# Seventeen of 25 node tiles reach their two experts through lists of places, with the expert's number in a register

## The chip, the core and the metric

The kernel runs on one core of a Trainium2 chip, as one launch. The metric is the device time of an execution in microseconds. Three runs of the kernel before took 2793.08, 2795.08 and 2800.14 us; their median is 2795.08. The profile comes from one further execution, which took 2804.75 us.

## The reference

The input is a graph of 3125 nodes with 512 features and 53,125 edges. A graph-attention network of two layers and a linear-attention mixer are added to the input; on the sum works a mixture of experts, and this is the part that the change is about:

```python
logits = xf @ Wg + bg                       # xf: layer norm of the 3125 rows
probs = softmax(logits, axis=-1)            # 8 experts
_, top_idx = top_k(probs, 2)
comb = probs * mask_of(top_idx)             # two weights a row are not zero
out = zeros_like(xf)
for e in range(8):
    h = gelu(xf @ W1[e] + b1[e])            # 512 -> 128
    y = h @ W2[e] + b2[e]                   # 128 -> 512
    out = out + comb[:, e:e + 1] * y
```

The reference computes every expert for every row and multiplies six of the eight results by zero. Everything is float32. The output is the sum plus this result.

## The kernel before

**Tiles and groups.** The nodes are sorted by their degree and cut into 25 tiles (`TILES`): 24 of 128 rows and one of 53. `FGROUPS` joins them in groups of four tiles; group 6 is the 53-row tile alone. The features of a group lie in `xT`, features by partition, rows along the free axis.

**The program.** A first part sorts the nodes and makes the tables of neighbours. Two attention layers follow, each with its feed-forward part and batch norm; they take the time up to about 2320 us of the profile. The last stage is the function `last`. The order of each engine's instructions is made by a scheduler from the order in which the program states them and from what they depend on, so that neighbouring pieces of the program interleave.

**The last stage.** `gates(t0, k)` is a generator that works on one group in five steps:

- four transposes a tile turn `xT` into rows, ScalarE copies them into `yall` (L1002), VectorE takes their statistics (L468, L469);
- two gathers a tile by indirect DMA on GpSimd fetch the rows of `base` and `xb` (L1012), GpSimd adds them (L1015), VectorE normalizes and adds (L1017, L1019) and takes statistics again;
- the normalized row `z` (L1028) is turned back into features (`to_features`: four transposes, and a copy that VectorE and ScalarE make in turns), and four matmuls with 8 columns give the gate's logits (L1033, L1035);
- softmax and the rank of each of the 8 weights (L1040 to L1058) leave two weights a row;
- the weights are transposed to `combT` (L1063, L1065).

`expert_sums(t0, k, ahead)` then adds the two biases `b2` by one matmul a tile (L1074, L1076), and for each of the 8 experts makes four matmuls of 512 columns into `ph` (L1080), a Gelu with the bias `b1` on ScalarE (L1083), and for each tile one matmul of 512 columns into `py` (L1087), which VectorE weighs and adds to `yall` (L1089). After each expert it asks the generator of the next group for one step, so that the gates of the next group stand beside the experts of this one. At the end GpSimd puts each tile's rows to their nodes' places in `out` by an indirect DMA (L1095). The groups come in the order 6, 5, 0, 1, 2, 3, 4 (L1100).

**Queues.** DMAs that `nc.sync` issues go out from SP, those of `nc.gpsimd` from GpSimd. In the last stage SP has only the loads of the experts' weights, issued ahead of it (`load_experts`), and GpSimd has the gathers, the additions of L1015 and the puts. Tiles of a pool have a fixed number of places (`bufs`), and a new use waits for the readers of the old one.

Of the kernel before, what the change touches and what calls it, by code (L numbers as in the profile page):

```python
# [53 lines left out]
assert FT == 25 and EP * EQ == NE and max(CAPS) < min(DEGS, PAD) and len(CAPS) == FT  # L54

# [354 lines left out]
def listed_layers(ctx: ExitStack, tc: tile.TileContext, rows,  # L410
# [553 lines left out]
    def load_experts(fp):  # L964
        w1t = fp.tile([128, NX, NP, FX], F32, name="w1t")
        w2t = fp.tile([FX, NX, D], F32, name="w2t")
        for e in range(NX):
            nc.sync.dma_start(w1t[:, e], w1[e].rearrange("(c p) f -> p c f", p=128))
            nc.sync.dma_start(w2t[:, e, :], w2[e])
        b2t = fp.tile([NX, D], F32, name="b2t")  # L970
        nc.sync.dma_start(b2t, b2)
        wgt = fp.tile([128, NP, NX], F32, name="wgt")
        nc.sync.dma_start(wgt, wg.rearrange("(c p) e -> p c e", p=128))
        bgt = fp.tile([P, NX], F32, name="bgt")
        nc.sync.dma_start(bgt, rows_by_partition(bg, 0, P))
        gt = fp.tile([P, D], F32, name="gt")
        nc.sync.dma_start(gt, rows_by_partition(rows, ROW_G, P))
        return w1t, w2t, b2t, wgt, bgt, gt


    def last(xT, w1t, w2t, b2t, wgt, bgt, gt):
        with tc.tile_pool(name="fin", bufs=1, reuse_waits="tile") as fp, \
                tc.tile_pool(name="fin_p", bufs=2, space=PSUM, reuse_waits="tile") as pp:
            yall = fp.tile([P, FT, D], F32, name="yall")
            puts, gated = [], {}

            def gates(t0, k):


                tiles = TILES[t0:t0 + k]  # L990
                mv = fp.tile([P, GT, 2], F32, name="mv1", bufs=2)
                mv2 = fp.tile([P, GT, 2], F32, name="mv2", bufs=2)
                prob = fp.tile([P, GT, NX], F32, name="prob", bufs=3)
# [32 lines left out]
                for i, (t, n) in enumerate(tiles):  # L1026
                    z = fp.tile([P, D], F32, name="z", bufs=3)
                    nc.vector.tensor_scalar(z[:n], yall[:n, t, :], mv2[:n, i, 0:1], sd[:n, i:i + 1],  # L1028
                                            op0=OP.subtract, op1=OP.mult)
                    to_features(pp, "tr", xT[:, :, t * P:t * P + n], z, n)  # L1030
                    pg = pp.tile([P, NX], F32, name="pg", bufs=1)
                    for c in range(NP):
                        nc.tensor.matmul(pg[:n], lhsT=xT[:, c, t * P:t * P + n], rhs=wgt[:, c, :],  # L1033
                                         start=(c == 0), stop=(c == NP - 1))
                    nc.vector.tensor_add(prob[:n, i, :], pg[:n], bgt[:n])  # L1035
                yield

                m = fp.tile([P, GT], F32, name="pm", bufs=2)
                wide = [P, GT, NX]
# [7 lines left out]
                rank = fp.tile(wide, F32, name="rank", bufs=2)  # L1047
                nc.vector.memset(rank, 0.0)
                for e in range(NX):
                    more = fp.tile(wide, F32, name="more", bufs=2)  # L1050
                    pe = prob[:, :, e:e + 1]
                    nc.vector.tensor_tensor(more[:, :, :e + 1], pe.to_broadcast([P, GT, e + 1]),
                                            prob[:, :, :e + 1], OP.is_gt)
                    if e + 1 < NX:
                        nc.vector.tensor_tensor(more[:, :, e + 1:], pe.to_broadcast([P, GT, NX - 1 - e]),
                                                prob[:, :, e + 1:], OP.is_ge)
                    nc.vector.tensor_add(rank, rank, more)
                nc.vector.scalar_tensor_tensor(prob, rank, 1.5, prob, op0=OP.is_lt, op1=OP.mult)  # L1058
                yield
                combT = fp.tile([NX, GT * P], F32, name="combT", bufs=2)  # L1060
# [5 lines left out]
                gated[t0] = prob, combT  # L1066

            def expert_sums(t0, k, ahead):
                prob, combT = gated.pop(t0)
                gs = slice(t0 * P, min(N, (t0 + k) * P))  # L1070
                w = gs.stop - gs.start
                for i, (t, n) in enumerate(TILES[t0:t0 + k]):
                    pb = pp.tile([P, 512], F32, name="pb", tag="py", bufs=3)
                    nc.tensor.matmul(pb[:n], lhsT=combT[:, i * P:i * P + n], rhs=b2t,  # L1074
                                     start=True, stop=True)
                    nc.vector.tensor_add(yall[:n, t, :], yall[:n, t, :], pb[:n])  # L1076
                for e in range(NX):
# [4 lines left out]
                    hT = fp.tile([FX, GT * P], F32, name="hT", bufs=3)  # L1082
# [8 lines left out]
                    next(ahead, None)  # L1091
                for _ in ahead:
                    pass
                for t, n in TILES[t0:t0 + k]:
                    puts.append(nc.gpsimd.indirect_dma_start(  # L1095
                        out=out, out_offset=bass.IndirectOffsetOnAxis(ap=node(t), axis=0),
                        in_=yall[:n, t, :], in_offset=None))


            groups = FGROUPS[-1:] + [FGROUPS[g] for g in FORDER if g != len(FGROUPS) - 1]  # L1100
            for _ in gates(*groups[0]):
                pass
            for i, g in enumerate(groups):
                expert_sums(*g, gates(*groups[i + 1]) if i + 1 < len(groups) else iter(()))
# [619 lines left out]
```

## Time and profile before

The profiled execution took 2804.75 us, and the span of its instructions is 2803.0 us; the median of the three runs is 2795.08 us.

| | whole span, 2803.0 us | last stage, 2330 to 2803 us |
|---|---|---|
| TensorE busy | 2398.1 us (86%) | 452.7 us (96%) |
| VectorE busy | 2054.1 us (73%) | 295.4 us (62%) |
| ScalarE busy | 1406.5 us (50%) | 108.4 us (23%) |
| GpSimd busy | 1414.4 us (50%) | 97.7 us (21%) |
| granted TensorE clock | 0.91 | 0.92 |
| DMA engines, mean share | | 12% |

A group's row in the profile names the line of the program, the engine, the operation, output and inputs, the shape and the count; then the busy time and the mean of one in ns; then the idle time just before these instructions and what ended it. A float32 matmul leaves two records. Records of TensorE overlap, so that the distance between two starts is what a matmul costs in a stream. A row of the timeline has the start, the length and the instruction, with equal neighbours merged. The granted clock is the share of full speed that the TensorE was given. "Landing" is the time from a DMA's issue to its arrival: 2.7 us for a put of L1095, 3.6 and 3.5 for the gathers of L1012, 2.7 for the write of a 256 KB tile by SP early in the program.

### The profile page before, as it was taken

What the parts mean: (1) busy time and instruction counts of PE and PEld (TensorE: products, weight loads), DVE (VectorE), ACT (ScalarE), POOL (GpSimd) and SP (SyncE); (2) the same over time, 40 slices, a digit from 0 to 9 for tenths busy, and PEclk for the clock granted to TensorE, in tenths of its full rate; (3) what the DMA queues carried; (4) which work ended last, traced back from release to release, by engine and by line L of the source; (5) the groups of instructions that cost most, each with busy time, mean ns of one, the idle gap of its engine ahead of it and who ended that gap; (6) DMA issues with size and microseconds to landing.
All of it is one profiled execution on the core that took longest, in us unless ns stands there. A gap on an engine that the chain in (4) does not pass through costs nothing. (4 is left out here: it accounts for less than half of the span.)

```text
span 2803.0 us, 30800 instructions
## 1 busy us (share of the span) xinstructions
PE 2398.1 (86%) x8935; PEld 1302.4 (46%) x8935; DVE 2054.1 (73%) x3186; ACT 1406.5 (50%) x5315; POOL 1414.4 (50%) x1153
## 2 busy tenths in 40 slices
PE   6987989889889876999697787979888486999998
PEld 3442445545455543344344555555555344444443
DVE  7810999999999985500679888989988566666663
ACT  1111568787776763200276767776767423222220
POOL 3362778888777770011657766676765323222100
PEclk9998999999999987999798888989999796999999
DMA  8434999999999984321869888989887441111000
GB/s 287 171 121 138 328 331 337 332 330 338 330 326 325 332 266 159 122 108 78 286 234 335 287 299 292 329 303 331 309 307 269 131 135 51 34 48 48 32 19 20
DMA packets 214478, 620.58 MB, mean 221 GB/s; under 512 B 48068, under 2 KB 53569, under 8 KB 210199
## 3 DMA queue, kind: packets, MB, share of 16 engines
q0 software_dynamic: 161696, 518.18, 52.4%
q1 hardware_dynamic: 50048, 95.36, 9.4%
q10 hardware_dynamic: 2556, 4.97, 0.5%
q8 instruction: 75, 1.23, 0.2%
q14 instruction: 103, 0.84, 0.1%
HBM read 543.80 MB, written 74.75 MB: 221 GB/s over the span
## 5 line engine op out<-in xcount | busy, mean ns | idle before, releaser
L583 POOL DMA_INDIRECT lane<-kvd,idx x906 | 1147.7, 1267 | 526.7 <-issue 179.7
L624 ACT ACTIVATE lane<-lane,sc 128x64 f32<-128x64 f32 x3888 | 945.4, 339 | 117.9 <-DVE sc L614 117.6
L588 DVE TENSOR_TENSOR lane<-lane,q 128x1024 f32<-128x1024 f32 (+1 forms) x464 | 549.0, 1193 | 161.8 <-DMA lane<-kvd,idx 146.7
L644 PE MATMUL agg<-ident,lane 128*128 128x128 f32 (+1 forms) x3272 | 531.6, 301 | 140.5 <-DVE lane L627 59.5
L644 PEld LDWEIGHTS agg<-ident,lane 128*128 128x128 f32 (+1 forms) x3272 | 424.2, 154 | 316.1 <-ACT lane L624 143.5
L589 DVE TENSOR_REDUCE sc<-lane 128x16 f32<-128x1024 f32 (+1 forms) x464 | 545.5, 1187 | 2.6 <-ACT lane L624 1.6
L627 DVE TENSOR_TENSOR lane<-lane,sc 128x1024 f32<-128x1024 f32 (+1 forms) x214 | 252.3, 1197 | 0.1
L1089 DVE SCALAR_TENSOR_TENSOR yall<-py,prob,yall 128x512 f32<-128x512 f32 (+1 forms) x200 | 148.8, 748 | 112.4 <-PE py L1087 100.8
L555 PE MATMUL pq<-wq,xg 128*128 128x512 f32 (+1 forms) x400 | 201.7, 634 | 18.5 <-ACT kt L734 12.2
L701 PE MATMUL po<-aT,wo 128*128 128x512 f32 (+1 forms) x448 | 194.2, 572 | 20.3 <-ACT aT L688 13.4
L1087 PE MATMUL py<-w2t,hT 128*128 128x512 f32 (+1 forms) x400 | 188.7, 610 | 1.8 <-ACT hT L1083 0.8
L1080 PE MATMUL ph<-xT,w1t 128*128 128x512 f32 x320 | 156.3, 630 | 0.0
L1095 POOL DMA_INDIRECT out<-yall,rec x25 | 25.0, 1001 | 252.3 <-DVE yall L1089 247.4
L1083 ACT ACTIVATE hT<-ph,colt 128x512 f32<-128x512 f32 (+1 forms) x56 | 35.4, 633 | 211.0 <-PE ph L1080 210.8
L494 POOL DMA_INDIRECT kvd<-kv,rec x25 | 24.7, 989 | 222.8 <-DVE kv L491 216.8
L491 DVE COPY kv<-pv 128x512 f32<-128x512 f32 (+1 forms) x25 | 17.3, 692 | 153.4 <-PE pv L488 153.4
L701 PEld LDWEIGHTS po<-aT,wo 128*128 128x128 f32 x448 | 80.3, 202 | 97.9 <-issue 64.9
L1087 PEld LDWEIGHTS py<-w2t,hT 128*128 128x128 f32 (+1 forms) x400 | 71.9, 189 | 101.3 <-issue 69.0
L555 PEld LDWEIGHTS pq<-wq,xg 128*128 128x128 f32 (+1 forms) x400 | 73.4, 199 | 92.8 <-issue 68.3
L372 ACT COPY kv<-pkv 128x512 f32<-128x512 f32 (+1 forms) x50 | 29.2, 585 | 163.8 <-PE pkv L370 136.4
L1012 POOL DMA_INDIRECT bt<-base,rec x25 | 26.8, 1072 | 160.1 <-DVE yall L1019 150.3
L370 PE MATMUL pkv<-wk,xT 128*128 128x512 f32 (+1 forms) x200 | 100.7, 637 | 5.8 <-ACT kv L372 5.8
(264 smaller groups left out, 3288.4 us busy)
## 6 DMA issues: line engine op xcount, KB each, us to landing
lane<-kvd,idx POOLq DMA_INDIRECT x906, 6.3
kvd<-kv SPq DMA_DIRECT2D x24, 512.0 KB, 2.7
zT<-ztd SPq DMA_DIRECT2D x48, 256.0 KB, 5.3
xmid<-xg SPq DMA_DIRECT2D x10, 1024.0 KB, 5.7
xT<-xmid POOLq DMA_DIRECT2D x10, 1024.0 KB, 10.3
xr<-in_x SPq DMA_DIRECT2D x24, 256.0 KB, 3.9
xb<-xo SPq DMA_DIRECT2D x24, 256.0 KB, 5.6
zd<-z SPq DMA_DIRECT2D x24, 256.0 KB, 2.7
```

What stands on the lines that cost most here:

```text
L370: nc.tensor.matmul(ps[:n], lhsT=xT[t][:, c, :n], rhs=wkv[name][:, c, :], start=(c == 0), stop=(c == NP - 1))
L555: nc.tensor.matmul(ps[:n], lhsT=of_place(t, c), rhs=wq[:, c, :], start=(c == 0), stop=False)
L583: gets.append(nc.gpsimd.indirect_dma_start(out=kv[:n, k, :], out_offset=None, in_=kvd[l][:, :], in_offset=bass.IndirectOffsetOnAxis(ap=idx ...
L588: nc.vector.tensor_mul(ks, ks, self.q[:n, None, :].to_broadcast([n, g, D]))
L589: nc.vector.tensor_reduce(self.sc[:n, :, j:j + g].rearrange("p h g -> p g h"), ks.rearrange("p g (h d) -> p g h d", h=H), AX.X, OP.add)
L624: nc.scalar.activation(v[:, k, h, :], v[:, k, h, :], AF.Copy, scale=self.sc[:n, h, j + k:j + k + 1])
L627: nc.vector.tensor_mul(v, v, self.sc[:n, :, j:j + g].rearrange("p h g -> p g h")[:, :, :, None] .to_broadcast([n, g, H, DH]))
L644: nc.tensor.matmul(self.agg[:, c * n:(c + 1) * n], lhsT=kv[:n, k, c * 128:(c + 1) * 128], rhs=ident[:n, :n], is_transpose=True, start=firs ...
L701: nc.tensor.matmul(ps[:, :w], lhsT=wo[:, kk, c * 128:(c + 1) * 128], rhs=aT[gi][:, kk, :w], start=(kk == 0), stop=(kk == NP - 1))
L1080: nc.tensor.matmul(ph[:, :w], lhsT=w1t[:, e, c, :], rhs=xT[:, c, gs], start=(c == 0), stop=(c == NP - 1))
L1087: nc.tensor.matmul(py[:n], lhsT=hT[:, i * P:i * P + n], rhs=w2t[:, e, :], start=True, stop=True)
L1089: nc.vector.scalar_tensor_tensor(yall[:n, t, :], py[:n], prob[:n, i, e:e + 1], yall[:n, t, :], op0=OP.mult, op1=OP.add)
```

## The change

Tiles 0 to 15 and tile 24 (`LISTED`, 2101 rows) no longer go through all experts. Groups 5 and 4 (`ALL_EXPERTS`), tiles 16 to 23, still do.

- While the gates of all other groups run, the eight experts of group 5 are stated between them, one after every third step of the gates. The bias term (L1074, L1076) has become the last step of `gates`. The weights and ranks of the listed tiles are kept in `lprob` and `lrank`, and their rows `z` are also written to DRAM (`zld`) by SP.
- `lists()` counts for each expert how many rows chose it, gives every choice a place (experts one after another, each beginning at a multiple of 128), and makes three tables: `placei`, the two places of each row; `which`, the row that stands at each place, by 34 one-hot matmuls; `experti`, the expert of each part of 128 places. There are 40 parts (`PARTS`: (2 x 2101 + 8 x 127) / 128, rounded down), whatever the data.
- Group 4 has its gates and three experts stated after that.
- `one_expert(part, e, which)`, 40 times: GpSimd gathers the 128 rows of a part, four transposes and a ScalarE copy make features of them, four matmuls of 128 columns and one for the bias `b1` make `ph`, ScalarE the Gelu, one more transpose and a VectorE copy turn `h`, one matmul of 512 columns makes `py`, VectorE copies it, SP writes it to DRAM (`yld`). The weights are addressed by a register `e`, loaded for eight parts at a time.
- Then come the other five experts of group 4, and at the end each listed tile fetches its two rows by two gathers (34 in all), weighs and adds them on VectorE and is put to `out`.

Buffers of `xT` whose content is no longer needed serve as room for these tables and rows. The three places of `z` also serve for `y1`, `hT` has two places in place of three and `combT` one in place of two. `b1t`, a copy of `b1` on one partition, comes by way of DRAM. The core of the diff:

```diff
+ALL_EXPERTS = [FGROUPS[STAY[0]], FGROUPS[4]]
+LISTED = [t for g in FGROUPS if g not in ALL_EXPERTS for t in TILES[g[0]:g[0] + g[1]]]
+NL = len(LISTED)
+PARTS = (2 * sum(n for _, n in LISTED) + NX * (P - 1)) // P
...
+                    if listed:
+                        r = (u0 + i) * P
+                        nc.sync.dma_start(zld[r:r + n, :], z[:n])
                     to_features(pp, "tr", xT[:, :, t * P:t * P + n], z, n)
...
-            def expert_sums(t0, k, ahead):
+            def all_experts(t0, k, prob):
...
                         nc.vector.scalar_tensor_tensor(yall[:n, t, :], py[:n], prob[:n, i, e:e + 1],
                                                        yall[:n, t, :], op0=OP.mult, op1=OP.add)
-                    next(ahead, None)
-                for _ in ahead:
+                    yield
+                for t, n in TILES[t0:t0 + k]:
+                    put(t, n)
+
+            def lists():
...
+                for j in range(2 * NL):
+                    low = room[:, j % 4 * P:(j % 4 + 1) * P]
+                    nc.vector.tensor_scalar(low, iota, digf[:, 0, j:j + 1], number[:, j // 2:j // 2 + 1],
+                                            op0=OP.is_equal, op1=OP.mult)
+                    nc.tensor.matmul(pw, lhsT=low, rhs=hot[:, j, :], start=(j == 0),
+                                     stop=(j == 2 * NL - 1))
+                which = fp.tile([P, PARTS], I32, name="which")
+                nc.vector.tensor_copy(which, pw)
...
+            def one_expert(part, e, which):
+
+                x1 = xT.tiles[0][:, part % 4, :]
+                nc.gpsimd.indirect_dma_start(
+                    out=x1, out_offset=None, in_=zld[:, :],
+                    in_offset=bass.IndirectOffsetOnAxis(ap=which[:, part:part + 1], axis=0))
+                x1T = xT.tiles[1][:, :, part % 4 * P:(part % 4 + 1) * P]
+                to_features(pp, "tr", x1T, x1, P, nc.scalar.copy)
+                ph = pp.tile([P, FX], F32, name="ph1", tag="ph", bufs=2)
+                for c in range(NP):
+                    nc.tensor.matmul(ph, lhsT=x1T[:, c, :], rhs=w1t[:, bass.ds(e, 1), c, :],
+                                     start=(c == 0), stop=False)
+                nc.tensor.matmul(ph, lhsT=ones[0:1, :], rhs=b1t[0:1, bass.ds(e, 1), :],
+                                 start=False, stop=True)
+                h0 = 8 * NL * NX + part % 2 * 2 * P
+                h1, h1T = (xT.tiles[3].rearrange("p c r -> p (c r)")[:, h:h + P]
+                           for h in (h0, h0 + P))
+                nc.scalar.activation(h1, ph, AF.Gelu_apprx_tanh)
+                pt = pp.tile([FX, P], F32, name="pt", tag="pg", bufs=1)
+                nc.tensor.transpose(pt, h1, ident)
+                nc.vector.tensor_copy(h1T, pt)
+                py = pp.tile([P, 512], F32, name="py", bufs=3)
+                nc.tensor.matmul(py, lhsT=h1T, rhs=w2t[:, bass.ds(e, 1), :], start=True, stop=True)
+                y1 = fp.tile([P, D], F32, name="y1", tag="z", bufs=3)
+                nc.vector.tensor_copy(y1, py)
+                nc.sync.dma_start(yld[part * P:(part + 1) * P, :], y1)
...
-            groups = FGROUPS[-1:] + [FGROUPS[g] for g in FORDER if g != len(FGROUPS) - 1]
-            for _ in gates(*groups[0]):
+            work = all_experts(*ALL_EXPERTS[0], weights(ALL_EXPERTS[0]))
+            ready = 0
+            for g in FGROUPS:
+                if g not in ALL_EXPERTS:
+                    for _ in gates(*g):
+                        ready += 1
+                        if ready % 3 == 0:
+                            next(work, None)
+            for _ in work:
                 pass
-            for i, g in enumerate(groups):
-                expert_sums(*g, gates(*groups[i + 1]) if i + 1 < len(groups) else iter(()))
+            placei, weight, which, experti = lists()
+            work = all_experts(*ALL_EXPERTS[1], weights(ALL_EXPERTS[1]))
+            for _ in range(3):
+                next(work)
+            RB = 8
+            for p0 in range(0, PARTS, RB):
+                es = nc.values_load_multi_w_load_instructions(
+                    experti[0:1, p0:p0 + RB], engines=[mybir.EngineType.PE], min_val=0, max_val=NX - 1,
...
+                for i, e in enumerate(es):
+                    one_expert(p0 + i, e, which)
+            for _ in work:
+                pass
+            for u, (t, n) in enumerate(LISTED):
+                for i in range(2):
+                    y1 = xT.tiles[3][:, (2 * u + i) % 4, :]
+                    nc.gpsimd.indirect_dma_start(
+                        out=y1[:n], out_offset=None, in_=yld[:, :],
+                        in_offset=bass.IndirectOffsetOnAxis(ap=placei[:n, u, i:i + 1], axis=0))
+                    nc.vector.scalar_tensor_tensor(yall[:n, t, :], y1[:n], weight[:n, u, i:i + 1],
+                                                   yall[:n, t, :], op0=OP.mult, op1=OP.add)
+                put(t, n)
             apart(puts, "rows of distinct nodes")
```

## The prediction

> **What bounds the kernel now.** I read four views in this order: the chain of waits, the busy times by stretch, the groups of instructions, and the timeline of the end. The chain of waits runs from 2336 us almost only over L1080, L1087 and L1074, the expert matmuls of the last stage. Four stretches of that stage (start and end, length, busy us and instructions of TensorE, its weight loads, VectorE, ScalarE, GpSimd; granted TensorE clock; DMA share; GB/s):
>
> ```profile
> 2330.00:2400.00 70.00, 61.11 (x215) 38.22 (x216) 47.48 (x144) 21.75 (x36) 23.19 (x20) 0.69 0.18 51
> 2452.00:2521.00 69.00, 68.92 (x205) 33.09 (x206) 46.38 (x107) 17.22 (x23) 17.53 (x17) 0.98 0.14 47
> 2521.00:2590.00 69.00, 68.93 (x205) 33.13 (x206) 46.16 (x107) 17.22 (x23) 17.65 (x17) 0.98 0.15 47
> 2660.00:2729.00 69.00, 68.93 (x206) 33.06 (x204) 45.69 (x103) 17.22 (x23) 3.88 (x4) 0.98 0.04 16
> ```
>
> A group of four tiles takes 69 us, TensorE is busy in all of it at nearly full clock, and VectorE only in 46. The gates of the next group are hidden behind the experts. Only the first stretch differs: gates with little expert work, VectorE at 68%, the clock at 0.69.
>
> ```profile
> L1087 PE MATMUL py<-w2t,hT 128*128 128x512 f32 x384 | 179.3, 606 | 1.1 <-ACT hT L1083 0.8
> L1080 PE MATMUL ph<-xT,w1t 128*128 128x512 f32 x320 | 156.3, 630 | 0.0
> L778 PE MATMUL ctxp<-vt,kt 128*128 128x130 f32 x192 | 29.3, 283 | 4.1 <-DVE vt L775 4.1
> L1089 DVE SCALAR_TENSOR_TENSOR yall<-py,prob,yall 128x512 f32<-128x512 f32 x192 | 142.9, 748 | 111.7 <-PE py L1087 100.4
> ```
>
> Each f32 matmul leaves two records. The start-to-start distance says more than the mean, since records overlap:
>
> ```profile
> 2485.13 0.64 PE L454 MATMUL tr<-ident,z 128*128 128x128 f32 x4
> 2485.60 1.02 PE L1087 MATMUL py<-w2t,hT 128*128 128x512 f32 x2
> 2486.46 0.95 PE L1033 MATMUL pg<-wgt,xT 128*128 128x8 f32 x8
> 2487.27 0.64 PE L454 MATMUL tr<-ident,z 128*128 128x128 f32 x4
> ```
>
> A 512-column record takes (2486.46 - 2485.60)/2 = 0.43 us, a record with 128 columns or fewer 0.10 (0.81/8) to 0.12 (0.47/4). I use 0.107, a quarter of 0.43.
>
> **What goes.** Four whole groups and the 53-row tile lose their experts. In the chain an expert of a whole group is one 3.43 us piece of L1080 and one 3.68 us piece of L1087: 4 x 8 x 7.11 = 228 us, and some 15 us for the last tile, all on the path. Had nothing come in its place, the stage from 2328 to 2803, 475 us, would lose half. But those experts are also what the gates hide behind.
>
> **What comes, in order of time.** Up to the last stage the instructions of each engine stand in the same order in both programs, so I start at 2328 us, where its first rows appear.
>
> *1. Gates with eight experts.* In the changed program's order the gates of groups 5, 0, 1, 2, 3 and 6 run with the eight experts of group 5 strewn between them. VectorE: 46.2 us a group, less 32 L1089 at 0.748 (23.9), leaves 22.3 for a group's gates; five groups 112, the last tile about 8 (eight 512-wide operations at 0.7, the rest small), group 4 as far as its rows z 17 (four times 2 x 0.682, 2 x 0.171, 0.772, 0.755, 0.691, plus two copies at 0.69), group 5's L1089 24: **161 us**. TensorE has some 115 us here at full clock. Neither fills the time; each waits for the other (z, transposes, copy, gate matmuls, softmax, pb). The nearest row is the first stretch, the same chain with VectorE at 68%. The other end is 84%, 471.65 us in the 560 us from 1700 to 2260, a stretch that keeps VectorE fed. There is less TensorE work in the way than in the first stretch, so I take 70%: **230 us** (bounds 192 and 237). A new wait is inside: a row z (three buffers) now waits for the write to zld of the tile three before. Such a write lands in 2.7 us, so the fourth z of a group waits about 1 us, and behind it on VectorE its copies and gate sums.
>
> *2. The lists.* On VectorE about 20 operations of 128x136 at 0.30 (between 0.188 for 128x32 and 0.69 for 128x512), 20 small ones at 0.17, one of 128x1360 at 1.5: 11 us. Then 34 one-hot rows, which with four places wait for the matmuls that read them; TensorE does 34 x 0.22 and, in between, seven expert matmuls at 0.86: 13.5 us. Together **24 us**, with no other work for VectorE.
>
> *3. From the lists to the parts.* On TensorE the gate matmuls and four L1080 of group 4 (6 us), VectorE's softmax and ranks (4.5), the transposes of the weights and combT (1.5), four pb (3.4), twelve py (10.3) stand before part 0's second matmul: **26 us**. The first gathers (1.3 us issue, 3.5 to landing) lie beside it.
>
> *4. Forty parts.* One part: 4 transposes, 4 x 2 records of ph, 2 for the bias, one transpose of h: 15 x 0.107 = 1.6; py 0.86; and 0.2 of waiting. A wait of TensorE for ScalarE and back costs the operation plus 0.4: ph of one matmul ahead leaves 0.23 us of gap today with a Gelu of 0.69. The program works on parts in pairs, and only the first Gelu of a pair (0.37 + 0.4, against 0.43 of cover) shows, 0.34 a pair. So 2.66 us a part, less 3 us already done in step 3: 103 us, and 109 at a clock of 0.95. ScalarE (0.59 + 0.37), VectorE (0.69 + 0.29) and GpSimd (1.3) stay under 2.66; the gathers have four places and two parts' time to land. [...]
>
> *5. The register.* Each of 240 matmuls has a register instruction before it, and five loads of eight registers stand in the stream. The trace has neither between matmuls. Below: nothing, if the queue ahead of the array covers it. Above: 0.2 us each, 48 us, about two of the small records it stands between. Four of the six sit among 0.2 us matmuls and little covers them: I take 0.05, **12 us**. [...]
>
> *6. The end.* All parts must have been written before the first row comes back: copy 0.7 and a write of 2.7, 3.6 us with the waits. Then GpSimd issues 34 gathers and 21 puts. Its pace (start, us, operation):
>
> ```profile
> 2791.77 0.97 POOL L1095 DMA_INDIRECT out<-yall,rec  x1 [59.09 <-DVE yall L1089]
> 2793.04 0.97 POOL L1095 DMA_INDIRECT out<-yall,rec  x1 [0.31 <-issue]
> 2794.32 0.97 POOL L1095 DMA_INDIRECT out<-yall,rec  x1 [0.30 <-DVE yall L1089]
> 2795.59 0.97 POOL L1095 DMA_INDIRECT out<-yall,rec  x1 [0.30 <-issue]
> ```
>
> That is 1.27 us each, 1.31 with the slower L1012 (1.061 against 1.001 us): 55 x 1.31 = 72 us. The five experts of group 4 that are left (36 us) hide behind it, not it behind them. The last put waits for its second row (2 us more), and from its end to the span's end 6.4 us pass today. Sum **84 us**, against 10 us after TensorE's last matmul now.
>
> **Sum.** 230 + 24 + 26 + 109 + 12 + 6 + 84 = 491 us against 475: **+16 us**. The span goes from 2803 to 2819, the profiled execution from 2804.75 to 2821, and, as the three runs have a median of 2795.08, I forecast **2811 us**, 0.6% slower. 243 us of matmuls leave; the parts take back half, and most of the rest is gates, lists and returns that nothing covers.
>
> **Rivals.** *VectorE keeps full in step 1.* For it: the order always puts the next group's statistics into the gaps of this one's softmax. Against: the first stretch. At 84% step 1 takes 192 us: 2773; with the register steps covered as well, about 2755. It breaks even at 214 us, VectorE at 75%.
>
> *TensorE goes cold or is held by its registers in the parts.* For it: 0.69 in the first stretch; many short waits; a third of the records are transposes. Against: 0.98 where it is over 95% busy, and the parts should be so at about 93%. At half clock 15 x 0.214 + 1.72 is about 5 us a part, +97: 2908. Cold half the time: 2860. Registers at 0.2 us: 2847.
>
> That the change doesn't do what it says is small: the transposes, parts and returns stand in the program's order as described, and 40 parts are run whatever the data.
>
> **From this the numbers.** The measurement can tell about 0.3% (8.4 us) from no change. Forecast 0.45 (own range 2787 to 2835, of which 0.17 lies under 2803.5), VectorE full 0.33 (2749 to 2786), TensorE slow 0.22 (2836 to 2908). Faster 0.33, same 0.17, slower 0.50. The range 2755 to 2875 leaves out the ends of both rivals.
>
> **What would show it.** Step 1: `which` ready at about 2582, VectorE near 70% before it. Step 4: pairs of parts some 5.6 us apart and a clock over 0.9. Step 5: TensorE gaps put down to issue between ph matmuls. Step 6: GpSimd back to back for about 72 us after the last part, TensorE idle in the second half. It is wrong if parts take over 3.5 us each, if the lists come before 2560, or if the returns start before the parts end.

## The result, and the profile after

The changed kernel takes 2825.71 us (median of 4 runs, 2819.87 to 2836.55), the kernel before 2797.02 (4 runs): a ratio of 1.0108, with a 95% interval of 1.0074 to 1.0142. By the medians it is 28.7 us slower, where +16 were forecast. The profiled executions have spans of 2823.7 and 2803.0 us, +20.7; their last stages differ by 23.5 us (505.3 against 481.8, the table below). What the medians differ beyond that is not in the stages of these two executions, and isn't explained.

These are the stretches of the changed kernel's last stage (columns as in the prediction: start and end, length, busy us and instructions of TensorE, its weight loads, VectorE, ScalarE, GpSimd; granted TensorE clock; DMA share; GB/s):

```profile
2328.00:2520.00 192.00, 147.36 (x524) 82.50 (x522) 141.88 (x419) 50.48 (x76) 83.40 (x74) 0.75 0.29 88
2520.00:2545.00 25.00, 7.58 (x28) 4.60 (x29) 24.36 (x105) 4.16 (x8) 2.14 (x3) 0.57 0.09 35
2545.00:2570.00 25.00, 25.00 (x85) 18.80 (x85) 11.19 (x33) 2.56 (x3) 0.00 (x0) 0.50 0.00 0
2570.00:2608.00 38.00, 37.89 (x111) 21.74 (x112) 16.91 (x51) 6.18 (x9) 6.72 (x7) 0.71 0.17 49
2608.00:2730.00 122.00, 121.56 (x660) 85.84 (x659) 37.47 (x81) 30.72 (x76) 31.43 (x33) 1.00 0.51 156
2730.00:2824.00 94.00, 33.69 (x74) 12.96 (x72) 38.46 (x54) 3.44 (x5) 59.29 (x55) 0.75 0.48 153
```

Before, one pattern filled the stage: TensorE busy for 69 of 69 us, at a clock of 0.98. Now each stretch has its own limit. The gates (first row) keep VectorE at 74% and TensorE at 77%; in the lists (second) VectorE works nearly alone; the one-hot rows (third) and the way to the parts (fourth) have TensorE busy without a gap, but at half clock for the first 42 us; the parts (fifth) fill it at full clock; in the end (sixth) GpSimd issues one transfer after the other, 59.29 us of operations and 0.3 between each two, and TensorE has little to do. In the groups of the stage the experts' rows have shrunk and the parts' stand beside them:

```profile
L1141 PE MATMUL py<-w2t,hT 128*128 128x512 f32 x128 | 71.3, 699 | 12.3 <-DVE yall L1143 11.5 <-ACT hT L1137 0.8
L1243 PE MATMUL ph<-w1t,xT 128*128 x320 | 47.2, 284 | 0.1
L1143 DVE SCALAR_TENSOR_TENSOR yall<-py,prob,yall 128x512 f32<-128x512 f32 x64 | 47.2, 747 | 19.3 <-PE py L1141 17.3
L1255 PE MATMUL py<-w2t,xT 128*128 x80 | 44.9, 644 | 0.4 <-DVE xT L1253 0.4
L1291 POOL DMA_INDIRECT xT<-yld,placei x34 | 36.2, 1066 | 30.6 <-DMA yld<-y 20.6 <-issue 9.4 <-DMA xT<-yld,placei 0.3
```

The records of py are 384 before and 128 + 80 now. The mean of L1141 went from 606 to 699 ns although nothing in it changed: the 64 in the gates, a stretch with a clock of 0.75, take 760 ns, the 40 in the end 616. One pair of parts in the timeline (start, us, engine, line, operation), the distances to be read from start to start:

```profile
2643.88 1.13 PE L1255 MATMUL py<-w2t,xT 128*128 x2
2644.84 1.05 PE L1243 MATMUL ph<-w1t,xT 128*128 x8
2645.83 0.48 PE L1245 MATMUL ph<-b1t,ones 1*128 x2
2646.24 0.71 PE L1243 MATMUL ph<-w1t,xT 128*128 x4
...
2648.97 1.04 PE L462 MATMUL tr<-ident,xT 128*128 128x128 f32 x8
2650.00 1.13 PE L1255 MATMUL py<-w2t,xT 128*128 x2
```

From one py to the same py of the next pair: 2650.00 - 2643.88 = 6.12 us for two parts, without a wait. And the end on GpSimd:

```profile
2732.68 0.95 POOL L1291 DMA_INDIRECT xT<-yld,placei  x1 [20.58 <-DMA yld<-y]
2733.93 0.95 POOL L1291 DMA_INDIRECT xT<-yld,placei  x1 [0.30 <-issue]
...
2804.33 1.57 POOL L1291 DMA_INDIRECT xT<-yld,placei  x1 [0.30 <-issue]
2806.20 1.00 POOL L1123 DMA_INDIRECT out<-yall,rec  x1 [0.31 <-issue]
2813.31 1.58 POOL L1123 DMA_INDIRECT out<-yall,rec  x1 [6.11 <-DVE yall L1294]
```

54 transfers in 74.5 us, 1.38 each, and then 6.1 us of waiting for the weighing of the last tile, whose second row was gathered at 2804.33.

### The profile page after: what moved, and what is told of

It is laid out like the page before. It is cut to its first block, busy times and chain, and to the rows that moved or that the text cites. A ratio compares the mean times of both kernels' runs of the same rounds, so it can differ in the third digit from the quotient of the medians.

```text
span 2823.7 us, 31795 instructions
## 1 busy us (share of the span) xinstructions
PE 2319.8 (82%) x9096; PEld 1306.3 (46%) x9096; DVE 2029.8 (72%) x3245; ACT 1394.9 (49%) x5341; POOL 1482.8 (53%) x1231
## 5 line engine op out<-in xcount | busy, mean ns | idle before, releaser
L652 PEld LDWEIGHTS agg<-ident,lane 128*128 128x128 f32 (+1 forms) x3272 | 417.4, 153 | 322.5 <-ACT lane L632 149.2
L1236 POOL DMA_INDIRECT xT<-zld,which x40 | 38.1, 954 | 151.2 <-PE tr L462 96.7
L728 PE MATMUL pq<-wmk,zT 128*128 128x512 f32 (+1 forms) x200 | 99.4, 616 | 6.8 <-ACT kt L742 4.7
L728 PE MATMUL pq<-wmp,mqT 128*128 128x512 f32 (+1 forms) x200 | 96.5, 624 | 5.1 <-ACT mqT L851 4.4
L728 PE MATMUL pq<-wmv,zT 128*128 128x512 f32 (+1 forms) x200 | 96.7, 599 | 1.9 <-DVE vt L781 1.2
L742 ACT ACTIVATE mq<-pq,hm 128x64 f32<-128x64 f32 (+1 forms) x200 | 59.4, 320 | 67.3 <-DVE hm L739 67.2
L378 PE MATMUL pkv<-wv,xT 128*128 128x512 f32 (+1 forms) x200 | 91.7, 599 | 0.0
L728 PE MATMUL pq<-wmq,zT 128*128 128x512 f32 (+1 forms) x200 | 91.5, 595 | 0.0
```

The source lines that it names most:

```text
L378: nc.tensor.matmul(ps[:n], lhsT=xT[t][:, c, :n], rhs=wkv[name][:, c, :], start=(c == 0), stop=(c == NP - 1))
L652: nc.tensor.matmul(self.agg[:, c * n:(c + 1) * n], lhsT=kv[:n, k, c * 128:(c + 1) * 128], rhs=ident[:n, :n], is_transpose=True, start=firs ...
L728: nc.tensor.matmul(ps[:n], lhsT=lhs(c), rhs=w[:, c, :], start=(c == 0), stop=(c == NP - 1 and bias is None))
L742: nc.scalar.activation(oh[:, h, :], ph[:, h, :], AF.Exp, bias=m[:n, h:h + 1], accum_out=s[:n, h:h + 1])
```

## The experiments

The stage is measured from its first transpose (L1044) to the end of the span, because the work ahead of it, which no version changes, took from 2308 to 2374 us in these executions. For the same reason the ratio is always against the kernel before on the same chip, whose medians lay between 2795 and 2850 us. "Gates" is the time to the first one-hot row, "rows" from there to the cast of `which`, "way" from the cast to part 0's transpose of h, "parts" to the last part's py, "end" to the end of the span, all from the profiled execution.

| kernel | ratio to before (95%) | stage | gates | rows | way | parts | end |
|---|---|---|---|---|---|---|---|
| before | 1 | 481.8 | | | | | |
| changed | 1.0108 (1.0074 to 1.0142) | 505.3 | 226.0 | 25.8 | 37.0 | 121.1 | 95.4 |
| e1 gates first | 1.0190 (1.0149 to 1.0232) | 538.1 | | | | | |
| e2 no register | 1.0043 (1.0021 to 1.0066) | 498.6 | 226.0 | 15.2 | 41.9 | 119.9 | 95.6 |
| e3 short tile first | 1.0076 (1.0051 to 1.0101) | 503.8 | 226.0 | 25.8 | 37.0 | 121.1 | 93.9 |
| e4 no returns | 0.9909 (0.9882 to 0.9937) | 459.2 | 227.3 | 25.9 | 37.3 | 121.0 | 47.7 |
| e5 extra matmuls | 1.0090 (1.0059 to 1.0122) | 507.1 | 226.2 | 25.7 | 38.2 | 121.0 | 96.0 |
| e6 two experts held | 1.0118 (1.0075 to 1.0161) | 507.2 | 227.9 | 24.0 | 38.1 | 121.1 | 96.1 |
| e7 group 4 last | 0.9988 (0.9967 to 1.0008) | 485.4 | 228.2 | 15.5 | 26.6 | 120.9 | 94.2 |
| e8 kept warm | 1.0066 (1.0049 to 1.0083) | 496.2 | 226.5 | 28.4 | 26.9 | 120.6 | 93.8 |
| e9 and short tile first | 1.0075 (1.0058 to 1.0092) | 498.0 | 226.2 | 28.4 | 26.9 | 120.5 | 96.0 |
| e10 gates under parts | 1.0036 (1.0007 to 1.0065) | 493.7 | 216.0 | 15.2 | 13.5 | 154.9 | 94.1 |
| e11 and extra matmuls | 1.0019 (0.9988 to 1.0050) | 486.2 | 216.1 | 15.2 | 13.6 | 147.7 | 93.6 |
| e12 gates spread | 1.0023 (1.0005 to 1.0042) | 487.6 | 216.1 | 15.2 | 13.7 | 149.2 | 93.4 |

**e1: the gates without cover, alone.** In the kernel before:

```diff
-            groups = FGROUPS[-1:] + [FGROUPS[g] for g in FORDER if g != len(FGROUPS) - 1]
+            groups = [FGROUPS[g] for g in FORDER if g != len(FGROUPS) - 1] + FGROUPS[-1:]
...
-            for i, g in enumerate(groups):
-                expert_sums(*g, gates(*groups[i + 1]) if i + 1 < len(groups) else iter(()))
+            others = (s for g in groups[1:] for s in gates(*g))
+            for g in groups:
+                expert_sums(*g, others)
```

Each expert takes three steps of `others` instead of one, and pb moves into the gates, as in the changed kernel.

> The kernel before with one part of the change: all gates first, with the eight experts of group 5 strewn among them, then the experts of the other groups with nothing beside them; no lists, no parts. Theory (lost cover): the gates' stretch has 160 us of VectorE work (166 of the changed kernel less 11 for its lists, plus 5 for the rest of group 4) at 77%, 208 us; then five groups at 8 x 7.11 = 57 us, the last tile 15, the end 10: 518 us in place of 475, +43 us, about 2840. Rival (gates cost the same wherever they stand, and the lists and returns ate the gain): within 10 us of before.

The stage took 56 us more than before, the ratio 1.019. Gates of whole groups, with eight experts among them, in the first row, and three of the groups without gates:

```profile
2335.00:2545.00 210.00, 161.65 (x580) 90.56 (x581) 153.74 (x454) 64.49 (x96) 72.79 (x64) 0.76 0.18 52
...
2640.00:2697.00 57.00, 57.00 (x129) 23.66 (x128) 24.11 (x33) 5.50 (x8) 3.88 (x4) 1.00 0.05 19
2697.00:2754.00 57.00, 57.00 (x129) 23.66 (x128) 24.11 (x33) 5.50 (x8) 3.88 (x4) 1.00 0.05 19
```

A group without gates takes the 57 us expected, 12 less than with them. The gates took 242 us (to the last pb at 2577.2), not 208: VectorE at 73% in this row, and TensorE's clock at 0.76. So the loss of cover by itself costs 56 us; the rival is out.

**e2: no register.**

```diff
-                es = nc.values_load_multi_w_load_instructions(
-                    experti[0:1, p0:p0 + RB], engines=[mybir.EngineType.PE], min_val=0, max_val=NX - 1,
-                    skip_runtime_bounds_check_because="a count of seven comparisons")[1]
+                es = [p * NX // PARTS for p in range(p0, p0 + RB)]
```

> The changed kernel with the expert of a part a constant (part/5) and no loads; this changes the output, since parts go through other experts than their lists belong to. Theory (register steps cost a little on TensorE: 12 us of my sum plus 6 for loads, of which the trace shows next to nothing for the loads): 40 parts lose 0.3 us each, pairs 5.5 us apart instead of 6.12, -12 us. Rival A (the longer pairs are longer records, and the register steps are covered by the queue ahead of the array): pairs stay within 0.1 of 6.12, 0 to -3 us. Rival B (0.2 us for each of 240): pairs under 4.0 us, -48 us.

The parts took 119.9 us instead of 121.1: rival A by its size; what covers the register steps isn't shown. All 240 register matmuls and five loads together cost 1.2 us. The other 5 us of the stage come from the order: without the loads seven ph of group 4 stand behind the one-hot rows instead of between them (rows 10.6 us shorter, way 4.9 longer).

**e3: the 53-row tile returned first.**

```diff
-            for u, (t, n) in enumerate(LISTED):
+            for v, u in enumerate([NL - 1, *range(NL - 1)]):
+                t, n = LISTED[u]
                 for i in range(2):
-                    y1 = xT.tiles[3][:, (2 * u + i) % 4, :]
+                    y1 = xT.tiles[3][:, (2 * v + i) % 4, :]
```

> The changed kernel with the returns of the 53-row tile first instead of last. Theory (at the end a gather of 53 rows lands late, 8 us after its issue, where those of 128 rows land in 3.3 to 3.6): the last put's wait falls from 6.1 to under 2 us, -4 to -8 us. Rival (the last gather is late whatever its shape, because the queue of 55 transfers has fallen behind GpSimd): the last put waits 5 us or more, 0.

The last put's wait fell from 6.11 to 2.17 us, but the end only by 1.5. The start of the returns shows where the rest went (GpSimd):

```profile
2775.57 1.56 POOL L1292 DMA_INDIRECT xT<-yld,placei  x1 [20.77 <-DMA yld<-y]
2777.43 1.56 POOL L1292 DMA_INDIRECT xT<-yld,placei  x1 [0.30 <-issue]
2779.30 0.97 POOL L1292 DMA_INDIRECT xT<-yld,placei  x1 [0.30 <-issue]
2780.57 0.97 POOL L1292 DMA_INDIRECT xT<-yld,placei  x1 [0.30 <-issue]
2784.76 0.95 POOL L1292 DMA_INDIRECT xT<-yld,placei  x1 [3.21 <-DVE yall L1295]
```

The first weighing began at 2783.74, 8.2 us after its gather of 53 rows was issued, with no gather ahead of it: the shape is late, not the place in the queue, and it takes GpSimd 1.56 us where 128 rows take 0.97. In the changed kernel the last gather of 53 rows is alone in flight from about 2809 to 2812, and the mean share of the 16 DMA engines (second number from the end) is 0.06; in the first row, where a put of 128 rows is beside it, it is 0.49:

```profile
2808.00:2809.00 1.00, 0.00 (x0) 0.00 (x0) 0.00 (x0) 0.00 (x0) 0.00 (x0) 0.50 0.49 195
2810.00:2811.00 1.00, 0.00 (x0) 0.00 (x0) 0.00 (x0) 0.00 (x0) 0.00 (x0) 0.50 0.06 25
```

With four places the fifth gather now waits for the first (3.21 us): the wait moved. The theory was right in its mechanism and wrong in its worth.

**e4: no returns.** The gathers and the weighing are left out of the last loop:

```diff
-                    nc.gpsimd.indirect_dma_start(
-                        out=y1[:n], out_offset=None, in_=yld[:, :],
-                        in_offset=bass.IndirectOffsetOnAxis(ap=placei[:n, u, i:i + 1], axis=0))
-                    nc.vector.scalar_tensor_tensor(yall[:n, t, :], y1[:n], weight[:n, u, i:i + 1],
-                                                   yall[:n, t, :], op0=OP.mult, op1=OP.add)
```

> The changed kernel without the 34 gathers of rows from the parts' results and their weighing; the listed tiles are put out without their experts' sums. Theory (GpSimd's issue of one transfer after the other sets the end): only the five experts of group 4 are left after the last part, 36 us, four puts and the way to the end, 48 us in place of 95, -47 us. Rival (the five experts on TensorE and VectorE set the end and the transfers lie beside them): -15 us or less.

The end is 47.7 us, 48 expected. TensorE then runs group 4's experts without the waits of 3.1 us for L1143 that they have behind the weighing, and four puts follow. In the changed kernel GpSimd's transfers set the end.

**e5: eight extra matmuls ahead of the one-hot rows.**

```diff
+                for _ in range(8):
+                    warm = pp.tile([P, 512], F32, name="warm", tag="py", bufs=3)
+                    nc.tensor.matmul(warm, lhsT=rooms[7][:, :P], rhs=xT.tiles[1].rearrange("p c r -> p (c r)")[:, :512],
+                                     start=True, stop=True)
                 hot = room[:, 4 * P:4 * P + 2 * NL * PARTS].rearrange("p (j q) -> p j q", q=PARTS)
```

> The changed kernel with eight more 512-column matmuls, whose result nobody reads, ahead of the one-hot rows, in the 10 us in which TensorE waits for the lists. Theory (TensorE's clock, 0.50 from 2530 to 2587, sets the pace of the one-hot rows and of the way to the parts): with the array at full clock the one-hot rows take 13 to 15 us in place of 25.8, and from the cast of which to the first part 26 to 28 in place of 37: -20 us in all, although work is added. Rival A (VectorE and the four places for one-hot rows set the pace): the stretch keeps its 25.8 us, -3 to +3. Rival B (matmuls with 40 columns and 8 columns between the others let the clock fall again, or it doesn't rise in time): +3 to +8 us.

Rows 25.7, way 38.2: nothing won. Stretches of this run, the clock being the third number from the end:

```profile
2584.80:2588.50 3.70, 3.69 (x5) 1.63 (x6) 3.63 (x16) 0.30 (x1) 0.00 (x0) 0.52 0.00 0
2588.50:2593.50 5.00, 5.00 (x13) 2.12 (x12) 4.56 (x22) 0.00 (x0) 0.00 (x0) 1.00 0.01 2
2595.20:2598.61 3.41, 1.77 (x14) 1.33 (x12) 3.41 (x8) 0.00 (x0) 0.00 (x0) 1.00 0.00 0
2597.00:2600.00 3.00, 2.59 (x16) 2.35 (x17) 2.88 (x10) 0.01 (x1) 0.00 (x0) 0.77 0.00 0
2600.00:2623.00 23.00, 23.00 (x71) 16.50 (x71) 8.85 (x26) 2.55 (x3) 0.00 (x0) 0.50 0.00 1
```

The extra matmuls raised the clock after 3.7 us. It fell again 1.4 us behind the first one-hot row (2597.22), at the end of a stretch in which TensorE was busy for only 1.77 of 3.41 us, since it had waited for the lists. It then stayed at half although TensorE was busy in 23.00 of 23 us. Rival A is out by the rows, in which VectorE is busy for 8.85 of 23 us; rival B is right in that the clock falls again, but its cost is 1.1 us and not 3 to 8, a size that rival A gave.

**e6: two experts of group 5 held back into the lists.**

```diff
-                        if ready % 3 == 0:
+                        if ready % 4 == 0:
...
-            for _ in work:
-                pass
-            placei, weight, which, experti = lists()
+            placei, weight, which, experti = lists(work)
+            for _ in work:
+                pass
```

with a `next(work)` in `lists` ahead of pn and of pw.

> The changed kernel with two of group 5's eight experts held back from the gates: one is stated ahead of the prefix matmuls of the lists, one ahead of the one-hot rows. Theory (in the gates VectorE and its waits set the pace, so an expert less there is worth the 3 us of its sums on VectorE; in the lists it keeps TensorE's clock up): gates 3 to 6 us shorter, one-hot rows 15 to 20 in place of 25.8, the way to the parts 28 to 37: -15 us. Rival (the experts' sums stand ahead of the lists' operations on VectorE and delay them by as much as the gates win, and the clock falls before the one-hot rows all the same): -3 to +3.

The rival: two experts fewer in the gates bring nothing (227.9 us to the first row, with the two experts' sums ahead of it on VectorE), and the clock is at 0.50 in the rows.

**e7: all of group 4's experts behind the parts.**

```diff
-            for _ in range(3):
-                next(work)
```

> The changed kernel with all eight experts of group 4 behind the parts, where three stood ahead. Theory (what stands ahead of the parts is on the path; behind them TensorE has room beside GpSimd's transfers): from the cast of which to the first part 37 falls by the twelve py (10 us at full clock) and the matmuls of their ph that stood there, and the one-hot rows lose 7 ph: from the first one-hot row to the first part 62.8 becomes 42; the end grows from 95 to about 98, since eight experts at 10.5 us each, as they run there now beside the weighing, take 84 of it. Sum -18 us. Rival (the experts at the end wait longer for VectorE, which is held in its order by rows not landed yet, and group 4's puts come last): the end grows by 20 us, 0 in all.

The stage is 19.9 us shorter, 18 expected, and the kernel as fast as the one before: 0.9988 (0.9967 to 1.0008). Rows and way went from 62.8 to 42.1 us, and the end, with three experts more in it, didn't grow:

```profile
2760.80:2855.00 94.20, 61.46 (x126) 23.56 (x124) 46.92 (x67) 5.51 (x8) 59.59 (x55) 0.90 0.49 152
```

TensorE is busy in 61 of the 94 us, where it was in 34, beside the same 59 of GpSimd.

**e8 and e9: holding the clock, and more places.** On top of e7 and e5, beside each one-hot matmul one of 128 columns:

```diff
+                    keep = pp.tile([P, 512], F32, name="keep", tag="py", bufs=3)
+                    nc.tensor.matmul(keep[:, :P], lhsT=low, rhs=upper, start=True, stop=True)
                     nc.tensor.matmul(pw, lhsT=low, rhs=hot[:, j, :], start=(j == 0),
```

and in e9 e3's order with eight places, `xT.tiles[2 + v // 2 % 2]`.

> Group 4's experts last (as in e7), the eight extra 512-column matmuls ahead of the one-hot rows (as in e5), and beside each of the 34 matmuls of 40 columns one of 128 columns whose result nobody reads. Theory (a stream of 40-column matmuls lets the clock fall even without a gap, and one with matmuls of 128 columns, as the parts are, holds it): clock over 0.9 from the first one-hot row on, the rows 13 us (34 x 0.346 of VectorE and the way to the cast) where e7 has 15.5, and from there to the first part 17 to 21 where e7 has 26.6: -8 to -12 us against e7. Rival (the clock falls in this stretch whatever the columns, because of the waits between VectorE and TensorE): the 34 extra matmuls at half clock make the rows 20 us, +5 against e7.

> As e8, and the returns of the 53-row tile stand first, with eight places for rows instead of four. Theory (in e3 the late landing of the 53-row gathers only moved to the front, where it held GpSimd for 3.2 us through the four places; with eight it holds nothing): the end 4 to 5 us shorter than in e8. Rival (GpSimd's transfers run out of something else than places when one lands late): no gain. In all, against the kernel before: 0.992 by the theories of e8 and e9, 1.00 by both rivals.

Both theories failed. In e8 the rows took 28.4 us. The clock falls at the fourth row:

```profile
2535.42 0.47 PE L1224 MATMUL keep<-upper,xT 128*128 128x128 f32 x2
2535.72 0.32 PE L1225 MATMUL pw<-xT 128*128 128x40 f32 x2
2535.86 0.76 PE L1224 MATMUL keep<-upper,xT 128*128 128x128 f32 x2
2536.41 0.49 PE L1225 MATMUL pw<-xT 128*128 128x40 f32 x2
```

From keep to pw 0.30 us, and in the next pair 0.55. So one matmul of 128 columns beside each row didn't hold the clock here. Here too the stretch before the fall had TensorE busy for 1.77 of 3.41 us. In e9 the fifth gather no longer waits, but the end was 96.0 us: its last puts waited 7.88 us for group 4's last sums. The last ph ahead of them ran in part at half clock, and py waited 3.28 us for VectorE; which of the two cost the gain isn't shown.

**e10 to e12: group 4's gates under the parts.** On top of e7:

```diff
-            work = all_experts(*ALL_EXPERTS[1], weights(ALL_EXPERTS[1]))
+            prob = None
+            late = gates(*ALL_EXPERTS[1])
...
                     one_expert(p0 + i, e, which)
-            for _ in work:
+                    if 2 < p0 + i:
+                        prob = next(late, prob)
+            for _ in all_experts(*ALL_EXPERTS[1], prob):
                 pass
```

e11 adds e5's eight matmuls behind the last one-hot row, and e12 also spreads the steps: `if p0 + i >= 12 and i % 4 == 0`.

> Group 4's gates move from ahead of the parts to between parts 3 and 8, and all its experts stand behind the parts, as in e7. Theory (VectorE sets the pace of the gates and has room under the parts, where it is busy in 37 of 121 us): from the stage's first transpose to the first one-hot row 228 us become about 206 (17 us of VectorE's work at 77%), the rows 15.5 become 14, from the cast of which to the first part 26.6 become 10 to 15 (a gather that lands in 5, transposes, ph, Gelu), the parts 121 become 132 to 140 (TensorE does 32 transposes, 64 short matmuls and pb, 10.5 us, and some pairs wait), the end stays 94: about 463 where e7 has 485, -22 us, ratio to the kernel before 0.990. Rival (nothing ahead of the parts now raises TensorE's clock, which is at 0.5 after the one-hot rows, and the parts' short matmuls don't raise it either): parts at 5 us each for as long as this lasts; if for half of them, +40 us, ratio over 1.01.

> As e10, and eight extra 512-column matmuls, whose result nobody reads, behind the last one-hot row, where TensorE waits for the first part's gather. Theory of the clock (back-to-back 512-column matmuls raise it, and matmuls of 128 columns then hold it): parts at full clock from the first, 3 to 8 us less than e10 if that starts at half clock, much more if it stays there. Rival (the parts raise the clock by themselves within a few parts): within 3 us of e10.

> As e11, but the five steps of group 4's gates stand four parts apart (behind parts 12, 16, 20, 24 and 28) instead of one behind the other, so that each wait of the gates for VectorE can lie under parts that are ready. Theory (in e11 the parts took 147.7 us against 121 and 10.5 of added work on TensorE because the steps followed each other so closely that TensorE waited for VectorE, and its clock fell): parts 132 to 138 us, the rest as in e11 (216, 15, 14 and 94): about 473 us, 12 less than e7 and 9 less than the kernel before, ratio 0.996. Rival (the 8-column gate matmuls let the clock fall wherever they stand): parts 145 us or more, as e11, ratio 1.002.

Gates and way came out near the forecast (216 and 13.5 us, where 206 and 10 to 15 were expected), but the parts gave most of it back: 154.9 us without the extra matmuls, 147.7 with them (7 less, inside the 3 to 8), and 149.2 with the steps spread, where e10 expected 132 to 140 and e12 132 to 138. Stretches of e12, two before the transposes of z (from 2629.47) and two around and after them:

```profile
2552.00:2585.00 33.00, 32.52 (x161) 21.26 (x160) 6.69 (x15) 8.87 (x19) 11.61 (x13) 0.97 0.52 149
2585.00:2620.00 35.00, 34.29 (x199) 24.79 (x198) 21.32 (x47) 16.05 (x31) 10.55 (x11) 1.00 0.50 161
2620.00:2640.00 20.00, 17.43 (x81) 13.77 (x80) 6.55 (x15) 2.44 (x6) 0.95 (x1) 0.73 0.24 79
2640.00:2660.00 20.00, 19.57 (x80) 14.39 (x81) 6.85 (x38) 7.32 (x13) 4.95 (x6) 0.67 0.29 92
```

The clock held while parts and the first gate steps ran. It fell at 2629.1, just ahead of the transposes of z and after waits of TensorE for VectorE and ScalarE of 0.4 to 1.3 us, and stayed at half to 2653. The time is that of e12's rival; its mechanism holds for the stay at half clock and not for the fall, if the count below is right. Of the versions that do the whole work none is faster than the kernel before; the fastest, e7, can't be told from it.

**What goes with the clock, counted in the profiles before and after.** Every whole stretch at one granted clock, half or full, lasts a multiple of 3.41 us in these two profiles (102 stretches in the changed kernel, 116 in the one before). So the time can be cut into windows of 3.41 us, whose ends are known from the clock's changes, and the work in one window set beside the clock of the next. Three windows of the kernel before, around the four pb of a group (L1074, which start at 2451.89):

```profile
2449.09:2452.50 3.41, 3.41 (x9) 1.32 (x8) 2.75 (x4) 0.00 (x0) 1.74 (x2) 1.00 0.15 56
2452.50:2455.91 3.41, 3.41 (x9) 1.33 (x8) 2.68 (x6) 0.00 (x0) 2.18 (x3) 1.00 0.47 183
2455.91:2459.33 3.42, 3.42 (x5) 1.35 (x4) 0.40 (x1) 0.00 (x0) 0.00 (x0) 0.50 0.18 68
```

TensorE is busy in all three without a gap. But 3.0 us of the second are pb, whose weights have 8 rows where the others have 128, and the third is at half clock. A count by columns and rows tells them apart: a record counts as its time at full clock by its columns (0.43 us for 512, 0.107 for 128, 0.034 for 40), times the share of 128 rows that its weights have, set at the end of the record, and the sum of a window is divided by 3.41 us. The last stages of the two profiles have 288 such windows. The 87 with a count under 0.34 were all followed by half clock, the 199 over 0.42 all by full clock, and the two between by one of each. One limit, 0.37, is right in 99% of all; the best limit on TensorE's busy time in 83%. (Both limits are fitted to these windows, and many windows are alike, as the kernels are.)

By this count the one-hot rows lie under the limit. Four of them and one ph take 3.41 us at half clock (2551.77 to 2555.18 in the changed kernel) and count 8 x 0.034 + 2 x 0.43 = 1.13 us, 0.33. With keep beside them (e8) a row counts 2 x (0.107 + 0.034) = 0.28 us in 0.85 us, 0.33 again. The falls in e5, e8 and e12 themselves came after windows in which TensorE was busy for 1.77, 1.77 and 1.62 us; the rows that follow in e5 and e8 count 0.33, and the clock stayed at half. No run here changed the count alone, so this is a regularity of the traces and not a test.

## Why the prediction was right, and where its sizes were off

The direction and its causes held: half of the removed matmuls come back as parts, and the rest is lost in stretches that nothing covers. e1 shows the gates' lost cover by itself (56 us), e4 the returns (48 us of the end), e7 the three experts ahead of the parts (20 us). The sum of 491 us from 2328 to the end was measured as 495.7. That it is so close is luck: inside it errors of some -31 us (the gates and lists -25, the parts with their registers -6) and +35 us (rows 12, way 11, end 11) nearly cancel.

- **Step 1 and the small operations of the lists** (230 and 11): 217 us to the first one-hot matmul at 2544.8, VectorE busy 166 us of it, 77%, where 161 + 11 of 241 us make 71%. This is the rival "VectorE keeps full" half way; its breakeven was 75%. It didn't decide, because steps 2 and 3 took back as much. What was left of the gates' time is in part the clock: the four pb of a group take up to 7.2 us of the chain of waits at half clock, where step 3 put down 3.4.
- **Step 2, one-hot rows** (13.5): 25.8. The term that failed is the cost of a matmul at full clock: TensorE was busy in all of it, at 0.50. Seven ph in it took 1.85 us each and not 0.86, and the rows alone 15.5 (e7).
- **Step 3, to the parts** (26): 37, for the same reason until 2587.
- **Step 4, parts** (109): 3.06 us each and not 2.66, at a clock of 1.00 and with no waits. The waits (0.2 a part) and the clock (0.95) were too dear, the records too cheap: ph 0.12 us each ((2645.83 - 2644.84)/8), a transpose 0.13 ((2650.00 - 2648.97)/8), the bias 0.21 ((2646.24 - 2645.83)/2), py 0.96 for two. The quarter of 0.43 that the forecast took was near, with 0.12/0.43 = 0.28.
- **Step 5, registers** (12 and 6): 1.2 us in all (e2). No run shows the 6 us that the sum has for the loads: a load of eight registers took TensorE's queue 0.83 us in the trace (L1281, median), and without loads and register instructions the parts were only those 1.2 us shorter.
- **Step 6, end** (84): 95. Transfers 1.38 us instead of 1.31 (+4), the last row 4 us later than put down, since it is one of 53 rows (e3), and 8.8 us after the last put instead of 6.4.

Of the signs named, the clock in the parts, GpSimd back to back for some 72 us (74.5), TensorE idle in the second half of the end came out; `which` came at 2570 and not 2582, the pairs 6.1 us apart and not 5.6, and no gap was put down to issue between ph matmuls. The rival "TensorE goes cold" came true at another place: in the lists, not in the parts.

Open: whether the count sets the clock, since no run varied it alone. One-hot rows at full clock were never had, so what they would be worth isn't shown. Returning two rows of a tile with one transfer, which would halve the gathers, wasn't tried.

## What to carry to other kernels

Before work is taken off the engine that sets the pace, write down what it covers: here 56 us of gates came out from under it, and 48 us of new returns found nothing to stand under. What must stay dense belongs where another engine sets the pace: three experts behind the parts cost nothing beside GpSimd's transfers, and 20 us ahead of them. TensorE was busy for 42 us without a gap at half clock, so read the clock's column beside the busy one in every stretch, and count columns and rows of the matmuls where it is low.

## What the runs showed of the hardware

- TensorE busy was not TensorE at full clock. In the changed kernel it was busy from 2544.8 to 2587 without a gap at 0.50, in a mix of 40-column, 8-column and 512-column matmuls. Whole stretches at one clock lasted multiples of 3.41 us, before and after, and in e5 the clock rose after 3.7 us of 512-column matmuls back to back. The profile's busy time doesn't tell the clock, as these 42 us show; in these two traces the clock goes with the columns and rows counted above.
- The clock fell without a gap too: in the kernel before, after a window of 3.41 us of which 3.0 were matmuls with 8 rows of weights. Under the parts it stayed at half for 20.5 us (e11) and 23.9 us (e12) around the gate matmuls.
- Addressing the weights of a matmul by a register cost next to nothing here: 1.2 us for 240 of them and five loads (e2).
- A matmul over one partition (the bias, 1x128) took 0.21 us a record in the parts, more than one over 128 partitions (0.12); without a register (e2) it took 0.21 too.
- The two indirect gathers of 53 rows landed 8.1 and 7.8 us after their issue, those of 128 rows in 3.6 (median). The mean share of the DMA engines was 0.06 while the last was alone in flight.
